# A four-layer scan and attention network: moving the copies of the carried state and of the summed output inside a hand-ordered round, and trading buffers for a fourth state tile

## The chip, the cores and the metric

The kernel runs on one core of one Trainium2 chip. The time is the device time of one launch in microseconds (us), the median of the runs given. TensorE is called PE in the profile, VectorE DVE, ScalarE ACT, GpSimd POOL and SyncE SP. SP issues nearly all DMAs of this kernel.

## What is computed

Four images of 56 x 56 tokens with 96 channels pass through four layers. Layers 0 and 1 each contain a selective scan of 192 channels by 16 states along four directions of the image. Layers 2 and 3 are a linear attention and a quantized feed-forward block. Cut to the part that the change touches, the reference is this, for each image, direction and channel d with its 16 states s:

```python
def step(h, inp):
    da_t, db_t, x_t, c_t = inp          # da = exp(dt * a), db = dt * b
    h = da_t * h + db_t * x_t[..., None]
    y_t = jnp.einsum('bds,bs->bd', h, c_t)
    return (h, y_t)
_, ys = jax.lax.scan(step, h0, xs)      # over 3136 tokens
return jnp.swapaxes(ys, 0, 1) + seq * D
```

The results of the four directions (rows forward and back, columns forward and back) are added up. Around the scans stand layer norms, projections, 3 x 3 convolutions, gates and the feed-forward blocks.

## The kernel before: how the work is staged

**Chunks and rounds.** A direction's 3136 tokens are cut into 7 chunks of 448. The 192 channels are two halves of 96 (e = 0, 1), and the 16 states are four quarters (q = 0 to 3). A round takes one chunk, one e and one q: 96 channels x 4 states lie as 3 groups of 128 partitions by 448 tokens. There are 2 layers x 4 images x 4 directions x 7 chunks x 8 = 1792 rounds, and `scans` (line 600) writes them out in one loop. The position in a chunk is r = 4e + q. "Vertical" means a direction along columns (orient 1): half of all chunks.

**A round n, engine by engine.** The order on PE, ACT, DVE and POOL is exactly that in which the Python code emits it (a manual schedule, line 1347). SP is ordered by the framework's scheduler.

- DVE: scan 0 of round n, scan 1, then the product of round n+1 (`products`, line 701: du x b for two groups, written into h), then scan 2 of round n (all scans: line 708).
- ACT: decay 0 of round n+1 (`decay`, line 659, exp into one of three PSUM tiles `da`, each free again when the scan of that group of round n is done), decay 1, then side work, then decay 2, then `kept(n)` (line 677: the last state of each group of h is stored as the carry), then `carried(n + 2)` (line 672: the carry of eight rounds before, which is the previous chunk, is copied into the edge columns of the h tile that round n+2 will use). The product of round n+2 waits for that copy.
- POOL: `begin(n + 1)` (line 689, the product for the third group), then `hc` = h x c for round n (line 754). There are three h tiles, so `carried(n + 2)` takes the tile of round n-1 and waits until POOL has finished `hc` of round n-1.
- PE: zero matmuls (`keep_busy`, line 765: as many as lift the PE work counted for this round up to WARM; they add zeros to y), then `add_up` (line 775) for round n-2: with q = 0 it first starts the sum y from the earlier directions' result Y or from the skip term (line 782), adds two zero matmuls, then sums hc over the states (line 786); then projections for later chunks (line 431); and last `spread_b(n + 2)` (line 593), which spreads b over the partitions into the one PSUM tile b, free when the product of round n+1 has read it. The product of round n+2 waits for it.
- y is one PSUM tile. After the fourth quarter, `keep_sums` (line 790) copies it to Y on ACT (line 793) and, for the last direction, has SP store it (line 798). In the kernel before this copy stands in the same round as the fourth `add_up`, on ACT ahead of decay 2. It falls in the rounds with r = 1 and 5, since `add_up` lags two rounds. The next `add_up` with q = 0 falls in r = 2 and 6.

**Side work.** All other layers' work is cut into small parts ("lanes") and put into two places of each round, C (after decay 0) and F (after decay 1), by a planner: `spend`, `half_round` and `room` (lines 976 to 987) count estimated ACT and PE time against limits. The lanes of a stage (an image of a layer, 224 rounds) start in its round 2 (line 1353). What is left after the last scan runs alone at the end. Some lanes switch ScalarE's function table and back.

**Loads for the scan.** Per chunk, SP loads four tiles cb (b and c of a quarter, line 531; `fetch` at 6, 5, 4 and 3 rounds before the chunk; 7 buffers), and per e a dt and a du (line 512). Convolution lanes load input windows (line 941, NWIN = 4 buffers, two per chunk in the layer-1 convolution, where up to two chunks are open).

Of the kernel before, what the change touches and what calls it, by code (L numbers as in the profile page):

```python
# [11 lines left out]
F32 = mybir.dt.float32  # L12
# [10 lines left out]
C = 96  # L23
# [4 lines left out]
NQ = 4  # L28
# [4 lines left out]
CS = 448  # L33
# [3 lines left out]
NCS = L // CS  # L37
RANK = (12, 6)
NW, LATE_NW = 13, 20
NWIN = 4  # L40

SPARE = (0.9, 2.4)
ACT_LIMIT, PE_LIMIT = 4.0, 7.0
# [1 line left out]
DEPTH, LATE_DEPTH = 3, 6  # L45


WARM, PER_P = 6.8, 1.6

ORDER = (((0, 0), (0, 1), (1, 0), (1, 1)), ((0, 1), (1, 0), (1, 1), (0, 0)))  # L50
WD = NE * 128 + NE * C + NE + NE * NQ * NG
# [113 lines left out]
class Net:  # L165
# [359 lines left out]

    def fetch(self, ch, q):

        t = self.sp.tile([128, 2, CS], F32, name="cb", bufs=7)
        rows = ch.cd.rearrange("(k n) t -> n k t", k=2)
        for s in range(4):  # L530
            self.nc.sync.dma_start(t[32 * s : 32 * s + 32], rows[q + 4 * s].partition_broadcast(32))
        ch.cb.append(t)

    def prepare(self, ch, o):

        nc = self.nc
        if o == -14:
            self.parameters(ch)  # L540
        elif o == -12:
            self.inputs(ch)
        elif o == -9:
            ch.cd = self.dram.tile([2 * NS, CS], F32, tag="cd", name="cd", bufs=3)
            nc.sync.dma_start(ch.cd, ch.cf[: 2 * NS])
        elif o == -5:
            self.times_u(ch)
            ch.dtd = self.park(ch.dtc)
        elif o == -4:
            ch.dud = self.park(ch.duc)  # L550
            self.spread_dt(ch, 0)
        elif o == -3:
            self.spread_du(ch, 0)
        elif o == 0:
            self.spread_du(ch, 1)
            self.spread_dt(ch, 1)
        if -6 <= o <= -3:
            self.fetch(ch, o + 6)

    def prepare_on_scalar(self, ch, o):  # L560

# [38 lines left out]
    def scans(self):  # L600

        nc, sp = self.nc, self.sp
        chunks = []
        for l in range(2):  # L610
            for i in range(NB):
                for n, (orient, rev) in enumerate(ORDER[l]):
                    for step in range(NCS):
                        ch = Step()
                        ch.l, ch.i, ch.orient, ch.rev, ch.step = l, i, orient, rev, step
                        ch.k = 2 * orient + rev if l == 0 else orient + 2 * rev
                        ch.c = NCS - 1 - step if rev else step
                        ch.n, ch.first = n, n == 0 and step == 0
                        ch.skip = n == 0
                        ch.last = n == 3 and step == NCS - 1  # L620
                        ch.cb, ch.dt, ch.du = [], [], []
                        chunks.append(ch)
        rounds = [(ch, e, q) for ch in chunks for e in range(NE) for q in range(NQ)]
        per = NE * NQ


        da = [self.psum.tile([128, 512], F32, name=f"da{g}")[:, : CS + 4] for g in range(NG)]
        for t in da:
            nc.vector.memset(t, 0.0)

        def steps(n):

            return [(ch, n - per * j) for j, ch in enumerate(chunks[max(0, n // per) : n // per + 3], max(0, n // per))]

        def on_tensor(n):
            for ch, o in steps(n):
                self.on_tensor(ch, o)

        def on_scalar(n):
            for ch, o in steps(n):  # L640
                self.prepare_on_scalar(ch, o)

        def project(n):
            for ch, o in steps(n):
                for e in self.projected(ch, o):
                    self.project_step(ch, e)

        for n in range(-14, 0):
            for ch, o in steps(n):
                self.prepare(ch, o)  # L650
            on_tensor(n)
            on_scalar(n)
            project(n)

        def decay(n, g):

            if n < len(rounds):
                ch, e, q = rounds[n]
                nc.scalar.activation(da[g][:, INNER], ch.dt[e][:, g], AF.Exp, scale=ch.par.na[:, e, q, g : g + 1])  # L659

        def column(t, at):

            return t[:, at : at + 2 * ROW + 1 : ROW]

        def carried(n):

            if n < len(rounds):
                ch, e, q = rounds[n]
                hs[n] = sp.tile([128, WIDE], F32, name="h", bufs=3)
                if not ch.step:  # L670
                    return
                nc.scalar.copy(column(hs[n], ROW if ch.rev else 1), ch.par.carry[:, e, q])  # L672

        def kept(n):
            ch, e, q = rounds[n]
            if ch.step < NCS - 1:
                nc.scalar.copy(ch.par.carry[:, e, q], column(hs[n], 2 if ch.rev else CS + 1))  # L677

        hs, bs = {}, {}

        def tokens(t):

            return self.groups(t, 2)[:, :, :CS]

        def begin(n):

            if n < len(rounds):
                ch, e, q = rounds[n]
                nc.gpsimd.tensor_tensor(tokens(hs[n])[:, 2], ch.du[e][:, 2], ch.cb[q][:, 1], ALU.mult)  # L689

        def spread_b(n):

            if n < len(rounds):
                bs[n] = self.spread_b(rounds[n][0], rounds[n][2])

        def products(n):

            if n < len(rounds):
                ch, e, q = rounds[n]
                b = bs.pop(n).unsqueeze(1).to_broadcast([128, 2, CS])  # L700
                nc.vector.tensor_tensor(tokens(hs[n])[:, :2], ch.du[e][:, :2], b, ALU.mult)  # L701

        def scan(n, g):
            ch, e, q = rounds[n]
            c = 1 if ch.step else 0
            way = slice(CS + 1 + c, 1, -1) if ch.rev else slice(2 - c, CS + 2)
            h = hs[n][:, g * ROW :]
            nc.vector.tensor_tensor_scan(h[:, way], da[g][:, way], h[:, way], 0.0, ALU.mult, ALU.add)  # L708

        carried(0)  # L710
        carried(1)
        spread_b(0)
        begin(0)
        self.exp_and_ln()
        self.tables = True
        for g in range(NG):
            decay(0, g)
        products(0)
        spread_b(1)
        late = []  # L720
        for n, (ch, e, q) in enumerate(rounds):
            r = NQ * e + q
            for c, o in steps(n):
                self.prepare(c, o)
            on_tensor(n)
            self.half_round()
            strided = [1.5 + 1.5 * ch.orient] * (r % NQ == 2)
            strided += [1.5 + 1.5 * c.orient for c, o in steps(n) for _ in self.projected(c, o)]
            self.spend((0.6, 0.7, 1.7, 0, 0, 0, 0.7, 0.6)[r], (0.4, 1.3, 1.3, 0, 0, 0, 0, 0.4)[r] + sum(strided))
            scan(n, 0)  # L730
            decay(n + 1, 0)
            yield "C", n, r
            scan(n, 1)
            decay(n + 1, 1)
            self.half_round()
            yield "F", n, r
            on_scalar(n)
            ended = late.pop(0) if len(late) == 2 else None
            if ended:
                self.keep_busy(ended[2])  # L740
            begin(n + 1)
            if ended:
                self.add_up(*ended)
                if ended[2] == NQ - 1:
                    self.spend(0.6, 0)
                    self.keep_sums(*ended[:3])
            project(n)
            products(n + 1)
            scan(n, 2)
            decay(n + 1, 2)  # L750
            kept(n)
            carried(n + 2)
            hc = sp.tile([128, NG, CS], F32, name="hc", bufs=3)
            nc.gpsimd.tensor_tensor(  # L754
                hc, tokens(hs[n]), ch.cb[q][:, 0].unsqueeze(1).to_broadcast([128, NG, CS]), ALU.mult,
            )
            late.append((ch, e, q, hc))
            del hs[n]
            spread_b(n + 2)
        for ended in late:  # L760
            self.add_up(*ended)
        self.keep_sums(ch, e, q)
        yield "C", len(rounds), 0
# [563 lines left out]
def tile_net(ctx: ExitStack, tc: tile.TileContext, aps, at, out):  # L1327
# [19 lines left out]
    with tc.manual_schedule(engines={E.PE, E.Activation, E.DVE, E.Pool}):  # L1347
        net.exp_and_ln()
        lanes = []
        for slot, n, r in net.scans():  # L1350
            p, u = divmod(n, rounds)
            net.slot, net.paced = slot, True
            if slot == "C" and u == 2 and p < 8:

                assert p > 5 or not lanes
                lanes.append(chain(*beside[p]))
                if p == 7:
                    lanes.insert(0, chain(net.fuse(3), net.attend(3)))
            if n > 1 and p < 8:
                lanes = go_on(lanes)  # L1360
# [22 lines left out]
```

## Time and profile before

| what | value |
|---|---|
| median of 3 runs (lowest, highest) | 8713.47 us (8693.99, 8729.88) |
| profiled execution: its own time | 8727.95 us |
| profiled execution: its span | 8725.9 us |
| DVE scans, line 708 | 5376, 1070 ns each |
| DVE products, line 701 | 1792, 1068 ns each |
| ACT copies of y, line 793 | 448, 758 ns each |
| ACT copies of the carry into h, line 672 | 1536, 192 ns each |
| zero matmuls, line 773 | 4780, 1321.9 us of PE in all |
| first product to the end of the last scan | 119.0 to about 8350 us |

A line of the profile's group table gives the line of the kernel, the engine, the operation, what is written and read, and how often; then the busy time in us and the mean of one in ns; then how long the engine stood idle just before these instructions, and what ended most of that. In the list of waits the three numbers are us in total, times, and the longest. A line of the timeline gives the start and the length in us, the engine, the line, and in square brackets the idle time before it.

### The profile page before, as it was taken

The page shows a single profiled execution, that of the slowest core. Times are in us where ns is not written, and L with a number is a line of the kernel's source. Part 1 is how long each engine was busy: PE and PEld are TensorE (multiplying, and loading weights), DVE is VectorE, ACT ScalarE, POOL GpSimd, SP SyncE. Part 2 cuts the span into 40 slices and gives each one's busy share as a digit, 9 for nine tenths or more (in the row PEclk, how much of TensorE's full clock was granted, in tenths as well). Part 3 has the DMA queues.
Part 4 walks back from the last instruction along what each step waited for, and adds up shares of the span by engine and source line. Part 5 has one row for each costly group of instructions (what it writes and reads, how often), then busy time and mean ns, then how long its engine had stood idle before and what let it go on. Part 6 is the DMA issues. An engine that isn't in the chain of part 4 may idle for free. (4 is left out here: it accounts for less than half of the span.)

```text
span 8725.9 us, 116604 instructions
## 1 busy us (share of the span) xinstructions
PE 7685.4 (88%) x33570; PEld 2758.7 (32%) x33570; DVE 7409.6 (85%) x7763; ACT 6182.8 (71%) x12807; POOL 7180.0 (82%) x3991
## 2 busy tenths in 40 slices
PE   7889888898889988898889989998899988998997
PEld 3332223232333223232232323333233333333344
DVE  5888988989888988889888898889988989889931
ACT  5777777676777767776677766667766777667746
POOL 4888988979888988889888898888888888889820
PEclk8888889888889889898888989888899888888986
DMA  5666777667667676667766676666766667666621
GB/s 150 176 179 168 182 175 176 160 153 185 166 167 172 163 183 171 167 168 171 176 167 167 162 183 167 157 154 169 181 164 152 159 165 191 153 151 159 173 72 46
DMA packets 944139, 1417.59 MB, mean 162 GB/s; under 512 B 169410, under 2 KB 936644, under 8 KB 942628
## 3 DMA queue, kind: packets, MB, share of 16 engines
q1 hardware_dynamic: 942720, 1408.34, 65.4%
q8 instruction: 263, 4.31, 0.2%
q14 instruction: 384, 3.15, 0.1%
q10 hardware_dynamic: 772, 1.80, 0.1%
HBM read 1141.42 MB, written 268.14 MB: 162 GB/s over the span
## 5 line engine op out<-in xcount | busy, mean ns | idle before, releaser
L754 POOL TENSOR_TENSOR hc<-h,cb 128x1344 f32<-128x1344 f32 x1792 | 4880.1, 2723 | 968.3 <-DVE h L708 748.9
L708 DVE TENSOR_TENSOR_SCAN h<-da,h 128x449 f32<-128x449 f32 (+1 forms) x5376 | 5497.5, 1070 | 27.3 <-POOL h L689 19.2
L659 ACT ACTIVATE da<-dt,na 128x448 f32<-128x448 f32 x5376 | 3386.0, 635 | 1577.3 <-DVE h L708 1511.5
L701 DVE TENSOR_TENSOR h<-du,b 128x896 f32<-128x896 f32 x1792 | 1913.1, 1068 | 863.9 <-ACT h L672 441.9
L786 PE MATMUL y<-hc,four 128*32 128x448 f32 x14336 | 1933.4, 615 | 46.1 <-POOL hc L754 45.7
L689 POOL TENSOR_TENSOR h<-du,cb 128x448 f32<-128x448 f32 x1792 | 1752.9, 978 | 119.1 <-ACT h L672 73.4
L773 PE MATMUL y<-w,zeros 128*96 128x448 bf16 x4780 | 1321.9, 394 | 0.0
L593 PE MATMUL b<-cf,sel 128*128 128x448 bf16 x1792 | 702.2, 392 | 350.0 <-DVE h L701 347.5
L773 PEld LDWEIGHTS <-zeros 128*96 128x96 bf16 x4780 | 613.5, 134 | 942.0 <-issue 778.7
L431 PE MATMUL pp<-U,wd 96*128 96x448 f32 x896 | 675.6, 843 | 23.5 <-ACT da L659 16.7
L477 PE MATMUL pp<-cf,wd 12*96 12x448 f32 (+1 forms) x896 | 504.8, 646 | 164.9 <-ACT dtc L487 86.8
L593 PEld LDWEIGHTS <-sel 128*128 128x128 bf16 x1792 | 179.2, 100 | 1329.3 <-issue 1329.3
L782 PE MATMUL y<-Y,ident 96*96 96x448 f32 x672 | 544.8, 900 | 31.4 <-ACT Y L793 31.2
L786 PEld LDWEIGHTS y<-hc,four 128*32 128x32 f32 x14336 | 295.3, 113 | 860.4 <-issue 579.5
L930 PE MATMUL ps<-win,dg 64*64 64x220 f32 (+9 forms) x1962 | 547.1, 481 | 6.4 <-DMA win<-x 6.4
L793 ACT COPY Y<-y 96x448 f32<-96x448 f32 x448 | 339.5, 758 | 257.5 <-PE y L786 256.3
L502 POOL TENSOR_TENSOR duc<-dtc,U 96x896 f32<-96x896 f32 x224 | 482.6, 2155 | 4.3 <-ACT dtc L489 4.3
L930 PEld LDWEIGHTS ps<-win,dg 64*64 64x64 f32 (+2 forms) x1962 | 243.9, 167 | 289.7 <-issue 242.5
L672 ACT COPY h<-carry 128x3 f32<-128x3 f32 x1536 | 294.3, 192 | 25.6 <-POOL hc L754 24.1
L487 ACT ACTIVATE dtc<-pp,wd 96x448 f32<-96x448 f32 x448 | 279.3, 623 | 27.3 <-PE pp L477 24.1
L838 PEld LDWEIGHTS ps<-avg,w 96*112 96x112 f32 (+1 forms) x1984 | 256.9, 194 | 114.1 <-issue 59.5
L677 ACT COPY carry<-h 128x3 f32<-128x3 f32 x1536 | 282.8, 184 | 9.7
(427 smaller groups left out, 6077.1 us busy)
## 6 DMA issues: line engine op xcount, KB each, us to landing
cb<-cd SPq DMA_DIRECT2D x3584, 112.0 KB, 4.2
dt<-dd SPq DMA_DIRECT2D x1792, 168.0 KB, 4.4
du<-dd SPq DMA_DIRECT2D x1792, 168.0 KB, 4.4
dd<-dtc SPq DMA_DIRECT2D x224, 336.0 KB, 3.1
dd<-duc SPq DMA_DIRECT2D x224, 336.0 KB, 3.1
U<-u SPq DMA_DIRECT2D x112, 168.0 KB, 4.5
z<-w SPq DMA_DIRECT2D x56, 224.0 KB, 3.4
u<-w SPq DMA_DIRECT2D x56, 224.0 KB, 3.8
```

The costliest lines, as they stand in the source:

```text
L431: self.nc.tensor.matmul(ch.ps.rearrange("p (a b) -> p a b", b=HS), ch.par.wx[:, e], self.in_order(self.U[e], ch.orient, ch.c * CS, CS), st ...
L477: self.nc.tensor.matmul(ch.pd, ch.par.wt[rows, C * e : C * e + C], ch.cf[rows], start=True, stop=True)
L593: self.nc.tensor.matmul(ps, self.sel[:, q], self.upper(ch.cf), start=True, stop=True)
L659: nc.scalar.activation(da[g][:, INNER], ch.dt[e][:, g], AF.Exp, scale=ch.par.na[:, e, q, g : g + 1])
L689: nc.gpsimd.tensor_tensor(tokens(hs[n])[:, 2], ch.du[e][:, 2], ch.cb[q][:, 1], ALU.mult)
L701: nc.vector.tensor_tensor(tokens(hs[n])[:, :2], ch.du[e][:, :2], b, ALU.mult)
L708: nc.vector.tensor_tensor_scan(h[:, way], da[g][:, way], h[:, way], 0.0, ALU.mult, ALU.add)
L754: nc.gpsimd.tensor_tensor(hc, tokens(hs[n]), ch.cb[q][:, 0].unsqueeze(1).to_broadcast([128, NG, CS]), ALU.mult,)
L773: self.nc.tensor.matmul(self.y[:C], self.zeros, self.some, start=False, stop=False)
L782: nc.tensor.matmul(o, w, self.in_order(a, ch.orient, ch.c * CS, CS), start=True, stop=False)
L786: nc.tensor.matmul(self.y[32 * n : 32 * n + 32], self.four, hc[:, g], start=n == 3, stop=n == 3 or q == NQ - 1,)
L930: self.nc.tensor.matmul(o[:, a - r0 : e - r0, x0:x1], diag[:, tap], win[:, a + dy - lo : e + dy - lo, x0 + dx : x1 + dx], start=n == 0, st ...
```

## The change

`carried(n + 2)` is emitted between decay 0 and decay 1 of round n, no longer after `kept(n)`, and h has four tiles. `keep_sums` is emitted in the round after its `add_up`, on ACT right behind decay 1, which puts it into rounds with r = 2 and 6. WARM goes from 6.8 to 6.4 (program: 4392 zero matmuls for 4780). To make room, window tiles go from 4 to 3 and cb tiles from 7 to 6, with the third and fourth `fetch` one round later. Lanes of a stage start in its round 3.

```diff
-NWIN = 4
+NWIN = 3
+FETCH = (-6, -5, -3, -2)
-WARM, PER_P = 6.8, 1.6
+WARM, PER_P = 6.4, 1.6
...
-        t = self.sp.tile([128, 2, CS], F32, name="cb", bufs=7)
+        t = self.sp.tile([128, 2, CS], F32, name="cb", bufs=6)
...
-        if -6 <= o <= -3:
-            self.fetch(ch, o + 6)
+        if o in FETCH:
+            self.fetch(ch, FETCH.index(o))
...
-                hs[n] = sp.tile([128, WIDE], F32, name="h", bufs=3)
+                hs[n] = sp.tile([128, WIDE], F32, name="h", bufs=4)
...
-        late = []
+        late, sums = [], None
...
             scan(n, 0)
             decay(n + 1, 0)
             yield "C", n, r
+            carried(n + 2)
             scan(n, 1)
             decay(n + 1, 1)
+            if sums:
+                self.spend(0.6, 0)
+                self.keep_sums(*sums)
             self.half_round()
             yield "F", n, r
             on_scalar(n)
             ended = late.pop(0) if len(late) == 2 else None
+            sums = ended and ended[2] == NQ - 1 and ended[:3]
             if ended:
                 self.keep_busy(ended[2])
             begin(n + 1)
             if ended:
                 self.add_up(*ended)
-                if ended[2] == NQ - 1:
-                    self.spend(0.6, 0)
-                    self.keep_sums(*ended[:3])
             project(n)
             products(n + 1)
             scan(n, 2)
             decay(n + 1, 2)
             kept(n)
-            carried(n + 2)
...
-            if slot == "C" and u == 2 and p < 8:
+            if slot == "C" and u == 3 and p < 8:
```

## The prediction

> **What bounds the kernel now.** I read the page first, then DVE's list of waits, then two stretches of the timeline.
>
> ```profile
> PE 7685.4 (88%) x33570; PEld 2758.7 (32%) x33570; DVE 7409.6 (85%) x7763; ACT 6182.8 (71%) x12807; POOL 7180.0 (82%) x3991
> ...
> L708 DVE TENSOR_TENSOR_SCAN h<-da,h 128x449 f32<-128x449 f32 (+1 forms) x5376 | 5497.5, 1070 | 27.3 <-POOL h L689 19.2
> L659 ACT ACTIVATE da<-dt,na 128x448 f32<-128x448 f32 x5376 | 3386.0, 635 | 1577.3 <-DVE h L708 1511.5
> L701 DVE TENSOR_TENSOR h<-du,b 128x896 f32<-128x896 f32 x1792 | 1913.1, 1068 | 863.9 <-ACT h L672 441.9
> ```
>
> Four engines are over 70% busy, so the share decides nothing. The scan stage does: it lasts from 119 to about 8350 us, 8231 us for 1792 rounds, 4.59 us each. A round without side work takes 3.95 us (7.02 to 10.97 in the second timeline below): three scans and a product, back to back on DVE. DVE is thus the floor, 1792 x 3.95 = 7078 us, and nearly all it loses beside its own side work is the 863.9 us that it stands idle before products (27.3 before scans). A product waits for two things: the carry copied into h (ACT, line 672) and b (PE, line 593):
>
> ```profile
> DVE h L701 <- ACT h L672: 441.9, 278, 6.0
> DVE h L701 <- PE b L593: 146.4, 102, 5.7
> ```
>
> How the first wait comes about:
>
> ```profile
> 1299.43 1.16 ACT L1049 ACTIVATE w<-ps,b 128x448 f32<-128x448 f32 x2
> ...
> 1300.61 1.28 ACT L817 ACT_TABLE_LOAD   x1
> ...
> 1301.90 0.64 ACT L659 ACTIVATE da<-dt,na 128x448 f32<-128x448 f32 x1
> ...
> 1302.56 0.19 ACT L672 COPY h<-carry 128x3 f32<-128x3 f32 x1
> ...
> 1302.79 1.09 DVE L701 TENSOR_TENSOR h<-du,b 128x896 f32<-128x896 f32 x1 [0.41 <-ACT h L672]
> ```
>
> A lane's two activations and a table load hold up decay 2; the carry copy is last in that row, and the product waits for it.
>
> The second stretch is a vertical round that begins near 4008.0 (r = 6), with no lane work:
>
> ```profile
> 4007.02 3.04 DVE L708 TENSOR_TENSOR_SCAN h<-da,h 128x449 f32<-128x449 f32 x3
> 4007.09 0.99 ACT L793 COPY Y<-y 96x448 f32<-96x448 f32 x1 [0.29 <-PE y L786]
> ...
> 4009.12 0.64 ACT L659 ACTIVATE da<-dt,na 128x448 f32<-128x448 f32 x1
> 4009.12 1.83 PE L782 MATMUL y<-Y,ident 96*96 96x448 f32 x2
> ...
> 4010.10 0.64 ACT L659 ACTIVATE da<-dt,na 128x448 f32<-128x448 f32 x1 [0.34 <-DVE h L708]
> ...
> 4011.61 0.96 PE L786 MATMUL y<-hc,four 128*32 128x448 f32 x8
> ...
> 4012.50 0.37 PE L593 MATMUL b<-cf,sel 128*128 128x448 bf16 x1
> ...
> 4013.94 1.05 DVE L701 TENSOR_TENSOR h<-du,b 128x896 f32<-128x896 f32 x1
> ```
>
> PE's chain from the start of y (9.12) to the end of b (12.87) takes 3.75 us, and b is ready 1.07 us before its product.
>
> **What the Trainium skill says.** "Perfetto Trace Analysis", section "Tensor Engine Instruction", has PE reorder only by pulling weight loads ahead, and ACT, DVE and GpSimd as strict FIFO. So a blocked matmul holds every later matmul. The trace agrees: the weights for b were loaded at 4007.94, its matmul ran at 4008.76. "TensorE: Matmul & The Clock Gate", section "What's actually happening", has the clock fall to half after an idle window of about 3.4 us; the zeros guard against that. The stretches of 400 us before the tail show 0.83 to 0.92, and whether the new waits trip it no line shows. "DMA: Bandwidth & Descriptors", section "Anatomy of one DMA", puts a semaphore wait on the issuing sequencer, so a blocked window load blocks the loads behind it on SP; SP's list of waits agrees (line 506 alone holds the queue 1925.9 us).
>
> **The carry copy, moved (gain).** A product then no longer waits for decay 2, kept and carried, but decay 2 is still needed by scan 2 right behind the product. So each wait shrinks by the product that now runs meanwhile and the two copies, 1.07 + 0.18 + 0.19 = about 1.4 us, and what is longer stays, now before a scan. Product by product in the trace, I count 305 waits that end within 0.15 us of the copy, 465 us (the list, by another rule, 278 and 441.9); the parts over 1.4 us sum to 123. Ceiling 465 - 123 = 342 us. ACT's lag is also carried on, so later decays come later: I take 290, floor 150. The copy itself costs nothing in its new place: decay 1 waits 0.34 us for scan 1 there, against 0.19; without that cover it is a moved 0.19 us, not an added one. With four tiles it waits for the hc of a round earlier; the old wait for POOL was 24.1 us and goes.
>
> **The copy of y, a round later (loss).** Before decay 2 of r = 1 and 5 it held ACT about 596 us (339.5 copying, 256.3 waiting for PE), of which 322 pushed decay 2; that gain is in the 290. What it adds is a new wait. y has one tile, and the add_up with q = 0 is in the round in which the copy now stands. On ACT the copy stands behind decay 1, which needs scan 1 of that round. In the stretch above: decay 1 ends at 10.74, the copy at 11.70, PE starts y at about 11.76 for 9.12, and with the same 3.75 us b is ready at 15.5, for a product due at 13.94. Stall: 1.6 us. Queued behind PE's blocked matmul are the zeros, the sums, b, and the lanes' matmuls of the next round. Horizontally the copy takes 0.53 and the chain 2.58 us (median in the trace): b at 11.30 + 2.58 = 13.88, just in time, 0. So 224 x 1.6 = 358 us (1.4 to 1.7 each: 314 to 380). Where ACT is late, decay 1 and the copy are later still: in these 448 rounds decay 1 ends on average 1.0 us later than in the undisturbed round, 0.45 after subtracting what the old copy pushed, 200 us at most; about half meets rounds that have no slack, +90. Against that, products at this place already wait for b in some vertical rounds, and the larger wait counts, not the sum: vertical waits there are 115 us, I take off 70.
>
> **The rest.** 388 fewer zeros x 0.277 us = 107 us of PE, in rounds that were being filled: 0 (-20 to +20, if PE lags or the clock falls). Two of four cb loads now wait for a recent hc instead of one: SP's 147.2 us of that wait may double, but the third is read four rounds (16 us) after its issue and lands in 4.2: 0. SP's store of Y moves with the copy: its wait is on SP alone, 0. Three window tiles: two open chunks want four, so SP can stand until PE has read one. By the program's waits one du load comes behind such a wait with no round to spare, others with two or more: landing 4.4 and a few queued loads at 1.7 make about 10 us (0 to 40). Lanes starting one round later leave PE 995 instructions after the last b for 974: 0.
>
> **Sum.** -290 + 358 + 90 - 70 + 10 = +98 on the profiled 8727.95 us, 1.1%; on the median of 8713.47, about 8810 us.
>
> **Rivals.**
> *Absorbed (faster).* The stall replaces what a group of four rounds already loses, in whatever round. Vertical groups lose 1.98 us on average (444 us in 224), and only a quarter lose nothing; filling each up to 1.6 us costs only 133 us by the trace. Then -290 + 133 = -157: about 8560. For it: while DVE stands, ACT and PE catch up. Against: the losses lie on ACT, and the stall comes at a fixed place behind it. It turns faster where over 168 of the new 448 us (358 + 90) are absorbed, the 70 included, since 448 + 10 - 168 = 290.
> *Cancelled.* Gain at its ceiling of 342, stall at its 314, 20 of lateness: about 8710.
> *Lag on top (slower still).* Only 200 us gained, lateness 120, no overlap, windows 30: +308, about 9020.
> *Not done:* excluded by the program's order, which has the copies where the diff says and PE's first matmul of y waiting for ACT.
>
> **Chances.** Forecast 0.50 (own range 8740 to 8900), absorbed 0.27, cancelled 0.15, lag on top 0.08. The range of 8570 to 8920 leaves out about half of the absorbed case and most of the last. Within 0.5%, about what a measurement of this kernel can tell from no change, lies the cancelled case.
>
> **What would show it.** Right: DVE's wait for ACT line 672 nearly gone; the wait for b (146.4 us) above 400, mostly in vertical rounds with r = 2 and 6; ACT's wait for y (256.3) gone; PE idle before line 782's successor until the copy ends; DVE waiting for decays before scan 2. Wrong: the idle time before products falls by 250 us or more (absorbed), or b is ready in vertical rounds, which would mean that PE's chain is shorter than 3.4 us or not in line behind the copy.

## The result, and the profile after

| | before | after |
|---|---|---|
| median of 4 runs each (lowest, highest), us | 8714.93 (8693.99, 8729.88) | 9080.94 (9078.49, 9091.50) |
| profiled execution: its own time / its span, us | 8727.95 / 8725.9 | 9078.49 / 9076.8 |
| granted PE clock, mean of the span | 0.878 | 0.847 |

The ratio of after to before is 1.0424 (1.0401 to 1.0447): 4.2% slower, 270 us above the predicted 8810 and outside the range. The sign was right.

These lines of the page of after answer to those of before (the line numbers are one or two higher):

```profile
PE 7790.8 (86%) x33182; PEld 2740.7 (30%) x33182; DVE 7417.6 (82%) x7763; ACT 6182.1 (68%) x12807; POOL 7195.7 (79%) x3991
...
L709 DVE TENSOR_TENSOR_SCAN h<-da,h 128x449 f32<-128x449 f32 (+1 forms) x5376 | 5503.3, 1073 | 65.0 <-ACT da L660 41.4
...
L702 DVE TENSOR_TENSOR h<-du,b 128x896 f32<-128x896 f32 x1792 | 1916.9, 1070 | 1131.0 <-PE b L594 1049.5
...
L775 PE MATMUL y<-w,zeros 128*96 128x448 bf16 x4392 | 1278.5, 409 | 0.0
L784 PE MATMUL y<-Y,ident 96*96 96x448 f32 x672 | 597.6, 982 | 599.1 <-ACT Y L795 558.7
...
L795 ACT COPY Y<-y 96x448 f32<-96x448 f32 x448 | 342.1, 764 | 27.9 <-PE y L788 27.4
```

The instructions of DVE and ACT in these lines got slower by less than 1% (a scan takes 1073 ns for 1070, a copy of y 764 for 758). DVE's idle time before products went from 863.9 to 1131.0 us and before scans from 27.3 to 65.0, in all +305 of the +351 us of span. Its cause changed. The wait for the carry copy (441.9) is gone, and the wait for b, 146.4 in the list of before, has become 1049.5. The 146.4 is too small. Counted by times, 228 products of the kernel before waited and then started within 0.15 us of the end of b, and they stood idle for 325 us; by the same count it is 540 products and 1050 us after. The list of before puts much of the difference down to `issue` and to decays.

Two PE lines give a first hint. In the kernel before they were these:

```profile
L773 PE MATMUL y<-w,zeros 128*96 128x448 bf16 x4780 | 1321.9, 394 | 0.0
...
L782 PE MATMUL y<-Y,ident 96*96 96x448 f32 x672 | 544.8, 900 | 31.4 <-ACT Y L793 31.2
```

There are 388 fewer zeros, but each now takes 409 ns for 394, and starting y takes 982 ns for 900. Both are PE work of fixed shape, so PE itself ran slower.

The list of waits names where PE stands in turn:

```profile
PE y L784 <- ACT Y L795: 684.2, 317, 5.8
```

Taking the products one by one shows what moved where. "At the place" are the products whose b comes behind the first add-up of a sum, a quarter of all (those for rounds with r = 0 and 4).

| DVE's idle time, us | before | after | difference |
|---|---|---|---|
| products at the place, vertical | 115 | 515 | +400 |
| products at the place, horizontal | 177 | 400 | +223 |
| all other products | 572 | 216 | -356 |
| third scans of a round | 27 | 65 | +38 |

By place, the change thus divides into -318 us where the carry and the old place of the y copy mattered, and +623 where the new place of the y copy matters.

### The profile page after: what moved, and what is told of

The parts are those of the page before. It is cut to its first block, busy times and chain, and to the rows that moved or that the text cites. A ratio compares the mean times of both kernels' runs of the same rounds, so it can differ in the third digit from the quotient of the medians.

```text
span 9076.8 us, 113287 instructions
## 1 busy us (share of the span) xinstructions
PE 7790.8 (86%) x33182; PEld 2740.7 (30%) x33182; DVE 7417.6 (82%) x7763; ACT 6182.1 (68%) x12807; POOL 7195.7 (79%) x3991
## 5 line engine op out<-in xcount | busy, mean ns | idle before, releaser
L709 DVE TENSOR_TENSOR_SCAN h<-da,h 128x449 f32<-128x449 f32 (+1 forms) x5376 | 5503.3, 1073 | 65.0 <-ACT da L660 41.4
L702 DVE TENSOR_TENSOR h<-du,b 128x896 f32<-128x896 f32 x1792 | 1916.9, 1070 | 1131.0 <-PE b L594 1049.5
L788 PE MATMUL y<-hc,four 128*32 128x448 f32 x14336 | 2008.1, 637 | 1.4 <-POOL hc L756 1.4
L775 PE MATMUL y<-w,zeros 128*96 128x448 bf16 x4392 | 1278.5, 409 | 0.0
L784 PE MATMUL y<-Y,ident 96*96 96x448 f32 x672 | 597.6, 982 | 599.1 <-ACT Y L795 558.7
L775 PEld LDWEIGHTS <-zeros 128*96 128x96 bf16 x4392 | 584.8, 140 | 886.5 <-issue 745.9
L478 PE MATMUL pp<-cf,wd 12*96 12x448 f32 (+1 forms) x896 | 483.8, 622 | 162.9 <-ACT dtc L488 106.3
L567 ACT COPY cf<-pp 64x448 f32<-64x448 f32 x448 | 235.8, 526 | 194.6 <-PE pp L587 187.5
L784 PEld LDWEIGHTS y<-Y,ident 96*96 96x96 f32 x672 | 116.0, 220 | 832.8 <-ACT Y L795 769.4
L795 ACT COPY Y<-y 96x448 f32<-96x448 f32 x448 | 342.1, 764 | 27.9 <-PE y L788 27.4
```

Source lines behind the costliest of these rows:

```text
L478: self.nc.tensor.matmul(ch.pd, ch.par.wt[rows, C * e : C * e + C], ch.cf[rows], start=True, stop=True)
L775: self.nc.tensor.matmul(self.y[:C], self.zeros, self.some, start=False, stop=False)
L784: nc.tensor.matmul(o, w, self.in_order(a, ch.orient, ch.c * CS, CS), start=True, stop=False)
L788: nc.tensor.matmul(self.y[32 * n : 32 * n + 32], self.four, hc[:, g], start=n == 3, stop=n == 3 or q == NQ - 1,)
```

## Where the stall of a vertical round comes from

The timeline of after, a vertical round with no lane work that begins at 4186.6 (start, length, engine; idle time before it in brackets):

```profile
4186.07 0.99 PE L478 MATMUL pp<-cf,wd 12*96 12x448 f32 x2
...
4188.67 0.64 ACT L660 ACTIVATE da<-dt,na 128x448 f32<-128x448 f32 x1 [0.23 <-DVE h L709]
...
4189.24 1.01 ACT L795 COPY Y<-y 96x448 f32<-96x448 f32 x1
...
4190.31 1.94 PE L784 MATMUL y<-Y,ident 96*96 96x448 f32 x2 [3.25 <-ACT Y L795]
...
4192.06 0.93 PE L775 MATMUL y<-w,zeros 128*96 128x448 bf16 x2
...
4192.92 1.72 PE L788 MATMUL y<-hc,four 128*32 128x448 f32 x8
...
4194.58 0.55 PE L594 MATMUL b<-cf,sel 128*128 128x448 bf16 x1
...
4195.17 1.09 DVE L702 TENSOR_TENSOR h<-du,b 128x896 f32<-128x896 f32 x1 [2.59 <-PE b L594]
```

In this round the copy does what the prediction said: it starts 2.6 us into the round behind decay 1, and PE starts y 3.7 us into the round (predicted: 3.76). But from there to the end of b PE takes 4.82 us, not 3.75. The eight sums take 1.72 us where they took 0.96 in the kernel before, b 0.55 for 0.37. So the stall is 2.59 us, not 1.6. The table of windows gives the granted clock (the column PEclk) before, during and after PE's wait:

```profile
core 0: us, PE busy (x) PEld busy (x) DVE busy (x) ACT busy (x) POOL busy (x), PEclk, DMA share, GB/s
4184.40:4186.60 2.20, 1.47 (x11) 0.33 (x3) 2.20 (x4) 1.36 (x3) 2.14 (x2) 1.00 0.00 0
4186.60:4190.30 3.70, 0.46 (x2) 0.00 (x0) 3.70 (x5) 3.14 (x7) 3.49 (x2) 0.89 0.00 0
4190.30:4195.10 4.80, 4.79 (x14) 1.30 (x15) 2.28 (x3) 3.13 (x7) 4.51 (x3) 0.50 0.50 139
```

While PE waits 3.25 us for the copy, its clock falls, and the whole chain to b then runs at half clock. Over all rounds in which a new sum starts the median chain went from 3.67 to 4.71 us (vertical) and from 2.58 to 4.14 (horizontal).

Theory: the copy's place behind decay 1 costs twice, once as the wait itself and once more through the clock that the wait lets fall. Rivals: the loss comes from the fewer zeros, from the buffers or lanes, or the low clock is a sign and no cause.

## The experiments

None of these kernels leaves out a part of the reference. Ratios are to runs of the kernel before on the same chip; the medians of these were 8728.88, 8730.12, 8738.11 and 8732.57 us on the four chips used.

**The parts alone.** `carry_only` is after, with the copy of y back behind its `add_up`:

```diff
-            if sums:
-                self.spend(0.6, 0)
-                self.keep_sums(*sums)
...
             if ended:
                 self.add_up(*ended)
+                if ended[2] == NQ - 1:
+                    self.spend(0.6, 0)
+                    self.keep_sums(*ended[:3])
```

> The kernel after, with the copy of y back in the round of its add_up (ahead of decay 2); the carry copy, the four h tiles, the smaller buffers, WARM 6.4 and the later start of the lanes stay. Theory (the loss is PE's wait for the late copy of y, made longer by a clock that halves while PE waits): b is again early, DVE's wait for b falls from 1049 us to under 250 and its wait for the carry copy stays near nothing; 8400 to 8500 us. Rival (smaller buffers, fewer zeros or ACT's lag cost the time): above 8800 us.

Measured: 8567.08 us, 0.981 (0.9791 to 0.9829). That is on the theory's side (the rival had above 8800), but short of its numbers: the wait for b is 485.1 us, where under 250 was expected. `sums_only` is before, with only the copy of y moved, and the lanes' start at round 3:

> The kernel before, with the copy of y alone moved to the following round behind decay 1 (lanes start in round 3); three h tiles, the carry copy last, old buffers, WARM 6.8. Theory: the whole loss and none of the gain, 9250 to 9400 us, with DVE waiting about 900 us or more for b. Rival (the loss needs the buffers or the fewer zeros): below 8900 us.

Measured: 9190.11 us, 1.0516 (1.0494 to 1.0538). Counted by times as above, products wait 948 us for b. So the move of y's copy makes the whole loss, and the rest of the change is a gain, though a smaller one than expected. Both effects were overestimated here; the separation by sign is clear. `buffers_only` takes the third part alone:

```diff
-NWIN = 4
+NWIN = 3
+FETCH = (-6, -5, -3, -2)
-WARM, PER_P = 6.8, 1.6
+WARM, PER_P = 6.4, 1.6
-... name="cb", bufs=7)
+... name="cb", bufs=6)
-        if -6 <= o <= -3:
+        if o in FETCH:
-            if slot == "C" and u == 2 and p < 8:
+            if slot == "C" and u == 3 and p < 8:
```

> The kernel before with nothing of the change but three windows, six cb tiles with their later loads, WARM 6.4 and the lanes' start in round 3; both copies and the three h tiles stay. Theory (the rest of the change is nearly nothing, as predicted): 10 us over the kernel before, from 0 to 40, so within 0.5% of it. Rival (the run with the carry alone lost a large part of its gain to the fewer buffers): 60 us or more over it.

Measured: 8697.72 us, 0.9956 (0.9941 to 0.9971). This fits neither the theory nor the rival: it is about 40 us faster, not slower. The carry and its fourth tile are then worth 0.981 / 0.9956 = 0.985, some 130 us by themselves. DVE's lists of waits show why it is so little, first that of `buffers_only`:

```profile
DVE h L702 <- ACT h L673: 427.9, 272, 6.0
DVE h L702 <- PE b L594: 117.1, 83, 5.7
```

and then that of `carry_only`:

```profile
DVE h L702 <- PE b L594: 485.1, 318, 5.9
DVE h L702 <- DMA du<-dd: 84.7, 18, 20.3
...
DVE h L709 <- ACT da L660: 70.6, 103, 1.8
```

The wait for the carry is gone, and that for b has grown, by the lists by 368 us. Counted by times it has grown by 181, from 305 to 486; the rest had other names in `buffers_only`. So b takes back part of what the carry gave: idle time before products falls by 253 us only (829.3 to 576.2). Third scans take another 107 back (27.7 to 135.1).

**The fourth tile of h.** `carry_three` is before, with the carry copy moved and three tiles kept, and the lanes' start at round 3. The copy is moved in every round, not only for r = 0 and 4 as the expectation puts it:

```diff
             yield "C", n, r
+            carried(n + 2)
             scan(n, 1)
...
             kept(n)
-            carried(n + 2)
...
-            if slot == "C" and u == 2 and p < 8:
+            if slot == "C" and u == 3 and p < 8:
```

> The kernel before, with only the carry copy of the rounds r = 0 and 4 moved behind decay 0, three tiles of h, the old buffers, zeros and windows. Theory: the gain of the moved carry needs the fourth tile, since with three the carry copy waits for the product with C of the last round, and decay 1 waits behind it: 8650 to 8800. Rival (that product is done early enough): the gain stays, 8560 to 8600.

Measured: 8950.66 us, 1.0261 (1.0234 to 1.0289), worse than the theory's number, and on its side. ACT's list of waits:

```profile
ACT h L672 <- POOL hc L754: 1377.7, 1123, 6.3
```

This wait was 24.1 us before. Decay 1 is queued behind it, and DVE stands 349.3 us before scans for 27.3, while its idle time before products falls by 145 us only (863.9 to 718.9). With three tiles the carry's move is a loss; with four it is a gain. (The other differences between this run and `carry_only` are those of `buffers_only`, 0.9956 by themselves.)

**The place of y's copy.** `sums_first` is after, with the copy still a round later, but ahead of decay 0 and not behind decay 1:

```diff
+            if sums:
+                self.spend(0.6, 0)
+                self.keep_sums(*sums)
             scan(n, 0)
             decay(n + 1, 0)
...
             decay(n + 1, 1)
-            if sums:
-                self.spend(0.6, 0)
-                self.keep_sums(*sums)
```

> The kernel after, with the copy of y still in the following round, but ahead of decay 0 in place of behind decay 1. It is then done about 1.3 to 1.8 us after the round begins, where it was 3.2 to 3.7. Theory: PE starts y about 1.9 us sooner and does not stand long enough to lose its clock, so b is early even in vertical rounds: 8350 to 8500 us. Rival (a copy in the following round is bad wherever it stands, since decay 0 and what follows come late): above 8700 us.

Measured: 8592.82 us, 0.9842 (0.9826 to 0.9857). Less gain than expected, but 488 us below after. The copy starts 0.78 us into the round in place of 2.74 (medians), and DVE is idle before products for 627.9 us in place of 1131.0. So it is standing behind decay 1 that makes the loss. Being a round later costs little: this run is 26 us above `carry_only`, and the intervals of the two ratios just touch. The expectation that PE would keep its clock holds in part only: the chain from y to b has a median of 2.59 us in horizontal rounds, but of 4.37 in vertical ones, where 47 of 224 chains ran under a mean clock of 0.55.

**The zeros and the lanes.** `warm68` is after with `WARM` at 6.8 again (4804 zeros for 4392), `carry_warm68` the same of `carry_only`, `carry_u2` is `carry_only` with `u == 2`, and `carry_no_two` is `carry_only` without `self.add_zeros(2)` in `add_up`.

> The kernel after with WARM back at 6.8, as before the change, so that the number of zeros is about that of before. Theory (the copy's place makes the loss, the zeros are nothing): 9080 within 40 us. Rival (fewer zeros let the clock fall): 8900 or less, and a granted clock back near 0.88.

Measured: 9068.68 us, 1.0393 (1.0369 to 1.0417). The zeros are not the loss.

> The kernel after with the copy of y back in its old place (as in the run of the carry alone, 8567), and WARM 6.8 in place of 6.4. Theory (the zeros are worth nothing): 8567 within 25 us. Rival (more zeros hold the clock up): 8540 or less; (zeros in the way of the tensor engine's work): 8600 or more.

Measured: 8602.57 us, 0.9856 (0.9831 to 0.9882) against 0.981. The rival with zeros in the way fits: the 399 more zeros cost some 35 us. The two intervals just fail to overlap, so this is near the limit of what can be told, but `buffers_only`, with 382 fewer, gained 40.

> The kernel after with the copy of y in its old place (8567), and the lanes of a stage starting in its round 2 again, as before the change. Theory (the lanes' start is worth nothing): 8567 within 25 us. Rival (the start one round later is a loss in eight stages): 8540 or less.

Measured: 8585.3 us, 0.9834 (0.9796 to 0.9871): the lanes' start makes no difference that can be seen.

> The kernel after with the copy of y in its old place (8567), without the two zeros between the start of y and the sums. There the product waits for b 485 us in all, 318 times, and the two zeros lie in the chain to b, 0.4 us at full clock and up to 0.93 at half. Theory (what is left after the carry's move is the chain to b): each of some 170 waits behind a first add-up gets up to 0.4 us shorter, 40 to 70 us: 8500 to 8530. Rival (the two zeros hold the clock up for the sums behind them): 8567 or more.

Measured: 8584.44 us, 0.9836 (0.981 to 0.9863): no gain. The wait for b is 476.4 us for 485.1, and the granted clock 0.864 for 0.879: with 896 zeros fewer in the chain, the clock is lower. This agrees with its rival, and doesn't prove it.

**Clock or sign: PE kept running during the wait.** Three kernels put more zeros into the old y, between the last sums and the copy, so that PE has work while it would wait. They differ from after in where and how many:

```diff
+    def close(self, n):
+        self.add_zeros(n - 1)
+        self.nc.tensor.matmul(self.y[:C], self.zeros, self.some, start=False, stop=True)
```

(The last sum leaves the accumulation open, `stop=n == 3` without `or q == NQ - 1`, and the zeros close it.) `fill_wait` calls it behind the C lanes:

```diff
             yield "C", n, r
             carried(n + 2)
+            if sums:
+                self.close(int(max(1.0, 7.5 - self.work + lanes)))
             scan(n, 1)
```

> The kernel after, with up to 7 more zero matmuls into the old y while PE would wait for the copy of y (fewer where a lane has PE work in that place); the copy then waits for them. The wait stays, the clock should not fall. Theory: PE's chain from y to b goes from 4.7 back to about 3.5 us in vertical rounds and from 4.1 to 2.5 in horizontal ones, some 400 us of waits go: 8650 to 8800 us. Rival (the wait alone costs the time, the clock is a sign of it): 9000 us or more, since PE has more to do.

Measured: 9222.6 us, 1.056 (1.0531 to 1.059). The expectation failed: the zeros stood behind the lanes' matmuls, and the copy had to wait for them:

```profile
ACT Y L803 <- PE y L783: 498.7, 247, 7.3
```

The clock did rise (0.885 for 0.847), but the copy came later still, on average 4.4 us into the round for 3.3. So this run does not tell the theory from its rival. `fill2` puts the zeros ahead of decay 0, and more than one only where no C lane is open:

```diff
+            if sums:
+                self.close(1 if self.live else 8 if r == 2 else 11)
             scan(n, 0)
```

> The kernel after, with extra zeros matmuls into the old y at the very start of a round, ahead of decay 0 (8 of them in r = 2, 11 in r = 6, only in groups without open C lanes, some 79 of 448 groups; elsewhere one closing matmul). They keep TensorE running while it waits for the copy of y, and are done before the copy can start. Theory (the wait halves the clock for the chain behind it, which is 1.1 to 1.3 us of each stall): in those rounds the stall before the product falls from about 2.5 to about 1.2 us where the add-up is vertical and from about 1.9 to about 0.6 where it is horizontal; 79 x 1.3 = about 100 us less than after: 8980, at least 8950. Rival (the low clock is a sign and not the cause; the wait for the copy alone makes the stall): the stalls stay, 9080 or a little more for the 1122 added matmuls.

Measured: 9016.13 us, 1.0345 (1.0311 to 1.0378): 65 us less than after, where 100 were expected, with 8980.2 to 9057.7 us in its four runs; the profiled one is the fastest. The profile tells more, since the very same rounds can be compared. The timeline of `fill2`, in the round of the same chunk as the one shown above:

```profile
4139.30 1.58 PE L778 MATMUL y<-w,zeros 128*96 128x448 bf16 x7
...
4140.72 0.36 PE L782 MATMUL y<-w,zeros 128*96 128x448 bf16 x1
...
4141.56 1.00 ACT L802 COPY Y<-y 96x448 f32<-96x448 f32 x1
...
4142.61 1.86 PE L791 MATMUL y<-Y,ident 96*96 96x448 f32 x2 [1.53 <-ACT Y L802]
...
4144.80 0.96 PE L795 MATMUL y<-hc,four 128*32 128x448 f32 x8
...
4145.69 0.37 PE L594 MATMUL b<-cf,sel 128*128 128x448 bf16 x1
...
4146.10 1.09 DVE L702 TENSOR_TENSOR h<-du,b 128x896 f32<-128x896 f32 x1 [1.21 <-PE b L594]
```

and its windows, first the wait and then the chain:

```profile
4138.90:4142.60 3.70, 2.17 (x10) 0.89 (x8) 3.70 (x5) 3.13 (x7) 3.48 (x2) 1.00 0.02 4
4142.60:4146.10 3.50, 3.49 (x15) 0.95 (x16) 2.29 (x4) 3.14 (x7) 3.23 (x3) 1.00 0.36 92
```

The copy still starts 2.66 us into the round (4138.90) and PE still cannot start y before 3.7. Only the clock is different, 1.00 for 0.50, and the stall is 1.21 us for 2.59. In all the filled groups (a group is the four rounds of one sum), the same ones taken in both kernels:

| | number | copy starts, median | chain y to b, median | mean stall | sum of stalls |
|---|---|---|---|---|---|
| vertical, after | 60 | 2.66 us | 4.83 us | 2.54 us | 152.6 us |
| vertical, `fill2` | 60 | 2.66 | 3.46 | 1.47 | 88.3 |
| horizontal, after | 20 | 2.66 | 4.66 | 1.96 | 39.1 |
| horizontal, `fill2` | 20 | 2.66 | 2.58 | 0.28 | 5.5 |

That is 98 us less in 80 groups, as the theory had it, with nothing changed in these groups but what PE does while it waits; the copy itself came 0.2 to 0.3 us later on average. The clock is a cause. `fill3` fills the other rounds too, with `5 if self.live` in place of `1 if self.live`:

> The run with zeros at the start of the round, with five of them instead of one in the other 369 groups too, in which C lanes are open. There the stalls still have a mean of 1.55 us (horizontal) and 2.46 us (vertical); in the filled groups they were 0.28 and 1.47. Theory (the clock falls during the wait, whatever else runs): if five zeros hold the clock as well as 8 or 11 do, up to 1.0 to 1.2 us in each, 370 to 440 us in all, less what the zeros (about 1 us of the tensor engine ahead of the lanes' matmuls) push: 8700 to 8900. Rival (in these groups the lanes make the stall, the clock is no matter, and the zeros push the lanes): 9020 or more.

Measured: 8959.7 us, 1.0264 (1.0223 to 1.0305). This lies between the theory and its rival: a gain of some 57 us on `fill2` (71 by the ratios), far less than expected. In the 202 other horizontal groups the chain came down from 4.07 in after to 2.58 us and the stalls from 329.8 to 259.7 us, although the copy came 0.46 us later on average. In the 164 other vertical ones five zeros left the chain at 4.19 us (after: 4.59), the copy came 0.49 later, and the stalls rose from 373.7 to 411.1. So with these zeros the clock comes back, in rounds with lanes, only at the price of a later copy; what share it has in their vertical stalls is not shown by an experiment.

## Why the prediction was wrong

**The bound and the signs: right in the main.** DVE's idle time before products made the difference. The wait for line 672 is gone, the wait for b is above 400, ACT's wait for y fell from 256.3 to 27.4, PE stands before y's first matmul, and decays are waited for before third scans (41.4 us). These are the signs listed for "right". One came in part only: the wait for b was to be mostly in vertical rounds, but 223 of the 623 us fell on horizontal ones, where a stall of 0 was forecast.

**"The carry copy, moved": 290 taken, 318 measured inside the whole change** (-356 +38 in the table of places). The size holds, but only in company: alone, the same step brings about 130 us (`carry_only` against `buffers_only`). There third scans wait 107 us more, 63 of them in the rounds with r = 2 and 6, whose decay 2 stands behind the old place of y's copy, and b takes 181 us back. The prediction did say that the relief of decay 2 was in the 290; it named decay 2 as what is next late, and missed b.

**"The copy itself costs nothing", with four tiles:** right, as far as the lists show: in after neither ACT stands idle before this copy nor a product behind it. `carry_three` shows that the step needs the fourth tile.

**"The copy of y, a round later": the failed step.** The prediction put +358 +90 -70 = +378; measured is +623. Its start of y was right to 0.1 us in vertical rounds (median 3.73 us into the round for 3.76). In horizontal ones it was to be 3.3, which came true where no lanes are open (3.23), but the median over all of them is 3.76. What failed above all is "with the same 3.75 us b is ready at 15.5", and "the chain 2.58 us ... just in time, 0" for horizontal rounds. Both chain times are those of a kernel in which PE mostly goes into y running, and they were used in one where PE has just stood still, for 3.25 us in the round shown. In `fill2`, where PE runs through most of the wait, chains of about the old length come back, 3.46 and 2.58, and so do stalls near those predicted: 1.21 us (median) for 1.6, and 0 (median) for 0. The failing term is thus the chain's length. It was 4.71 and 4.14 (medians), and the excess over 378 is 245 us. Of these, the filled groups account for 98 and the horizontal groups of `fill3` for 70 at least. The rest isn't settled by an experiment between the clock and a late copy.

The traces say more on it. Sorted by the clock granted during it, the chain of a vertical round takes 3.46 us where the mean is 0.95 or more (34 rounds of after) and 4.83 where it is under 0.55 (101 rounds). In the kernel before the same two figures are 3.45 (107 rounds) and 4.81 (31). An estimate of what the longer chains took: subtract from each stall what its chain exceeds 3.75 us (vertical) or 2.58 (horizontal), but no more than the stall. That is 421 us in after and 86 in the kernel before. The difference of 335 us is enough for the whole excess, if nothing else had moved, which is not shown.

The Trainium skill has this case: "TensorE: Matmul & The Clock Gate", section "HAM oscillation — how this bites in real kernels", tells of a short burst of matmuls behind a wait that is longer than the window, so that every next burst starts at half clock. The trace agrees on the half clock, with 0.50 in the 4.8 us behind the wait. It doesn't agree on the length: the wait of 3.25 us is shorter than the window of about 3.4 us, and the last section shows long chains behind much shorter pauses. The prediction cited a section of the same page, had PE start y 2.64 us later than before (11.76 for 9.12), and then put no price on the new wait: "whether the new waits trip it no line shows". Its range had to contain that price, and the trace of before had it: the 31 vertical chains of 4.81 us at half clock.

**The rivals.** *Absorbed* is refuted for the copy in this place. The stall was larger than predicted, not absorbed. *Lag on top*, 9020, came nearest, by luck: the gain was not 200, as it assumed. It has a share in the lateness. On average the copy starts 0.7 us (horizontal) and 0.5 us (vertical) later than in an undisturbed round, where the "+90" stood for about half of 0.45.

**"The rest": +10 taken, about -40 measured** (`buffers_only`). The zeros were put at 0 (-20 to +20); by `carry_warm68` against `carry_only` having fewer of them gains about 35 us. In after itself more of them make no difference that can be told (1.0393 against 1.0424, intervals overlap). The loads, windows and lanes showed no loss.

**The best version.** `carry_only`: 8567.08 us, 0.981 (0.9791 to 0.9829) of before, faster than both kernels. It keeps the carry's move with the fourth tile and the buffers, and leaves y's copy where it was.

## What to carry to other kernels

When a change makes PE wait, price the work behind the wait anew, at half clock, and don't take it from a trace in which PE arrived running. To tell the two costs of a wait apart, give PE harmless work during it and change nothing else. Put that work early enough that it is done before the awaited instruction could start, or it delays that one, as in `fill_wait`. Before a removed wait is counted as a gain, look for the next one to arrive in the same place, and for the buffer that the earlier issue needs.

## What the runs showed of the hardware

The clock of PE has two values in these traces, 1.0 and 0.5. In the round of after shown above it fell 2.4 us after PE's last matmul: a mean of 0.89 over the 3.70 us means full clock for the first 2.9. It fell 327 times in the kernel before and 418 times in after. In all fourteen traces every stretch at one clock lasts a whole multiple of 3.41 us, the last one of a trace apart, which the end cuts short.

Pauses shorter than 3 us went with long chains too. In after, vertical rounds sorted by PE's longest pause in the 5 us before y starts have a median chain of 3.46 us with under 0.5 us (50 rounds), 4.27 with 0.5 to 1 (14), 4.64 with 1 to 1.5 (31), and 4.75 to 4.83 with more (129). In `fill2` a pause of 1.53 us behind a burst of zeros left it at 3.46. So the single pause doesn't decide alone. What ran before it may count, and so may where it falls between the moments, 3.41 us apart, at which the clock can change; no run here separates the two.
